# Moving the second block's x load, two table copies, a short index list and one weight copy in the prologue of a CIN kernel

## The chip, the cores and the metric

The kernel runs on one core of one Trainium2 chip. Its time is the device time of one execution in microseconds (us); a kernel's time is the median over several runs. The engines are TensorE (PE, with its weight loads PEld), VectorE (DVE), ScalarE (ACT), GpSimd (POOL) and SyncE (SP). Transfers are issued from ACT, SP and POOL and carried by 16 DMA engines.

## The reference

The model is a compressed interaction network of three layers on `x`, which has 1024 samples, 39 fields and 64 embedding elements. Each layer multiplies its input with the fields, pair by pair and element by element, and mixes the products with a weight matrix:

```python
def _cin_layer(Xk, X0, W, b):
    O = W.shape[0]
    Hk, Fdim = (Xk.shape[1], X0.shape[1])
    Wr = W.reshape(O, Hk, Fdim)
    return jnp.einsum('bhe,bfe,ohf->boe', Xk, X0, Wr) + b[None, :, None]

for W, b in ((W0, b0), (W1, b1), (W2, b2)):
    Xk = _cin_layer(Xk, X0, W, b)
    outs.append(Xk.sum(axis=-1))
cin_output = jnp.concatenate(outs, axis=-1)
return cin_output @ fc_w.T + fc_b
```

W0 is 64 x 1521, W1 and W2 are 64 x 2496. All is float32 and the output is 1024 x 1.

## The kernel before

The pairs of fields are symmetric, so each unordered pair (and each field with a constant row of ones) needs one product. The kernel lays the pairs out over 128 partitions. For each of 32 blocks of samples (2048 columns each, 32 samples by 64 elements) five tiles of 128 rows, `rt[n % 2][:, 0..4]`, hold fields in five different orders. A product `(n, c)` of two of these tiles (`PAIRS`, six of them, c = 0 to 5; line 217, DVE) covers 128 pairs, and a smaller product `(n, 6)` of the tiles U and V (line 219) covers the rest for two blocks at once. PE multiplies each product with a weight chunk `wa[:, c]` (line 557 for c below 6, lines 577 and 588 for the rest) in four quarters of 512 columns, each in two passes, and collects a block in four PSUM banks. At the end of a block ACT and DVE finish the banks (lines 605 to 618).

The order of work is written out by hand: a list `steps` of the products, DVE computing the product four steps ahead of PE (`AHEAD`).

How the tiles are filled: `load(n)` (line 166) copies one block of `x` in 1248 pieces of 256 bytes into a table `xd` in DRAM; a table holds two blocks with, for each, a row of ones behind the 39 fields (`fill_ones`, line 362). `roll(n)` (line 176) makes POOL gather the five tiles of block n from the table by `lists` (line 172; 1 MB each), and `roll_small` gathers U and V (0.5 MB each) by the last two columns of `lists`. Block 0 is special. Its samples arrive as two halves in `xh` (line 249, ACT's queue). Tiles 0 to 3 are gathered straight from the halves, eight gathers of 0.5 MB (lines 383 to 385). Between the fourth and the fifth of them POOL issues `load(1)` (line 387). SP copies the halves on into the table (line 389, two copies of 156 KB). Tile 4 is gathered from the table (`roll(0, (4,))`, line 390), then U and V and the five tiles of block 1 (lines 469 and 470).

The weights are prepared in the prologue. ACT's queue carries W2, the first half of x, W0, W1 and the second half, in this order. PE turns and combines them into PSUM; ACT copies four pieces of W0 into `both` (line 459); DVE transposes four pieces of W1 out of PSUM into `flat` (line 489, called T below), copies of which fill the rest of `both`. From `both` DVE adds up the weight rows (`pairs`, line 524), PE transposes them (line 541) and ACT copies them to `wa` (lines 542 and 543). The masks for W1 (`v2`, line 448) and the integer lists of U and V (lines 465 to 468) are small DVE steps ahead of T.

The products of block 0 for c = 0, 1, 2 are split: their first 1024 columns need the first half's gathers only, the second 1024 columns those of the second half. After them come products (0, 3), (0, 4) and on over all 2048 columns; (0, 4) and (0, 5) are the ones that read tile 4.

## Time and profile before

| what | value |
|---|---|
| median of 3 runs | 734.55 us (734.49 to 734.55) |
| the profiled execution's own time | 734.99 us |
| its span, first to last instruction | 733.2 us |
| PE busy | 727.5 us (99%) |
| DVE busy | 638.9 us (87%) |
| POOL busy | 377.6 us (51%) |
| ACT busy | 167.7 us (23%) |
| granted TensorE clock | 1.000 |
| first product pass of PE (line 557) | at 17.02 us of the span |

A row of the page's fifth part gives a line, an engine, what is written and read, the count, the busy time with the mean of one instruction, and the idle time of the engine just ahead with what ended it. In the timeline and in the chain each row begins with the start in us from the span's start and the duration in us. A row that ends in `x4` stands for four instructions. "DMA to landing" is the time from the start of a DMA instruction until its transfer has landed.

### The profile page before, as it was taken

To read this page: it belongs to the slowest core of one execution; us is meant where nothing else is said; L and a number is where in the kernel's file an instruction comes from. 1 tells how busy PE (TensorE), PEld (TensorE's weight loads), DVE (VectorE), ACT (ScalarE), POOL (GpSimd) and SP (SyncE) were. 2 spreads that over 40 slices of the span, in tenths; PEclk is the share of its full clock that TensorE was granted. 3 is DMA by queue.
4 is the path that set the end of the run, shared out by engine and by line. 5 is a ranking of instruction groups with operands and counts; after the bars stand their busy time and mean duration, and the time that the engine had idled before them with its cause. 6 is when DMAs were issued, how large, how long until landed. Compare 5 with 4: busy or idle time off the path is not lost.

```text
span 733.2 us, 6352 instructions
## 1 busy us (share of the span) xinstructions
PE 727.5 (99%) x2377; PEld 314.9 (43%) x2377; DVE 638.9 (87%) x520; ACT 167.7 (23%) x241; POOL 377.6 (51%) x254
## 2 busy tenths in 40 slices
PE   9999999999999999999999999999999999999998
PEld 4344444444444444444444444444444444444443
DVE  6998889988889888898988889888898888889885
ACT  3332121222212222121221212221122221212222
POOL 6858754537555455654547545455654447535300
PEclk9999999999999999999999999999999999999999
DMA  8999967779585796757778676886767876566700
GB/s 264 419 296 381 377 263 276 282 286 323 223 279 238 287 354 261 264 236 265 310 286 299 236 286 228 313 347 224 274 244 276 314 286 259 201 270 245 287 0 1
DMA packets 65979, 197.23 MB, mean 269 GB/s; under 512 B 40109, under 2 KB 40174, under 8 KB 45980
## 3 DMA queue, kind: packets, MB, share of 16 engines
q0 software_dynamic: 28784, 185.56, 65.5%
q1 hardware_dynamic: 35464, 9.28, 5.5%
q10 hardware_dynamic: 1700, 1.99, 0.9%
q8 instruction: 18, 0.29, 0.2%
q14 instruction: 13, 0.11, 0.0%
HBM read 196.76 MB, written 10.60 MB: 283 GB/s over the span
## 4 chain that ended last, share of the span: by engine, by line
PE 97%; DMA 1%; POOL 1%; DVE 1%; issue 0%; ACT 0%; DVEq 0%
PE po L557 90%; PE po L577 4%; PE po L588 2%; DMA r<-xh,lists 1%; POOL r L172 1%; PE idle L276 0%; PE pv L399 0%; DVE p L217 0%; POOL xd L166 0%; PE tr L541 0%; DVE g L607 0%; DVE sums L629 0%; ACT z L605 0%; PE small L320 0%; DVE blocks L420 0%
## 5 line engine op out<-in xcount | busy, mean ns | idle before, releaser
L557 PE MATMUL po<-p,wa 128*128 128x512 f32 x1536 | 665.9, 594 | 0.7 <-DVE p L217 0.5
L217 DVE TENSOR_TENSOR p<-r 128x2048 f32<-128x2048 f32 (+2 forms) x197 | 434.4, 2236 | 74.2 <-PE po L557 72.7
L557 PEld LDWEIGHTS po<-p,wa 128*128 128x128 f32 x1536 | 289.6, 190 | 371.5 <-issue 348.5
L172 POOL DMA_INDIRECT r<-xd,lists x156 | 299.6, 1920 | 289.9 <-issue 275.2
L605 ACT ACTIVATE z<-po,columns 64x512 f32<-64x512 f32 x128 | 87.4, 683 | 375.0 <-PE po L588 220.1
L607 DVE SCALAR_TENSOR_TENSOR g<-po,b0s,z 64x512 f32<-64x512 f32 x128 | 95.9, 749 | 9.3 <-ACT z L605 5.3
L600 ACT COPY g<-r 39x1024 f32<-39x1024 f32 x64 | 66.7, 1043 | 149.2 <-DVE sums L618 120.4
L618 DVE TENSOR_REDUCE sums<-g 103x16 f32<-103x1024 f32 x62 | 75.6, 1220 | 2.1
L172 POOL DMA_INDIRECT u<-xd,lists x16 | 30.3, 1891 | 5.0 <-issue 4.6
L172 POOL DMA_INDIRECT v<-xd,lists x16 | 29.7, 1854 | 4.9 <-issue 4.9
L577 PE MATMUL po<-p,wa 32*64 32x512 f32 x512 | 31.6, 600 | 0.0
L219 DVE TENSOR_TENSOR p<-u,v 128x1024 f32<-128x1024 f32 x16 | 19.5, 1217 | 0.0
L577 PEld LDWEIGHTS po<-p,wa 32*64 32x64 f32 x512 | 9.4, 131 | 20.2 <-issue 20.2
L588 PE MATMUL po<-u,wa 32*64 32x512 f32 x256 | 17.0, 587 | 0.0
L172 POOL DMA_INDIRECT r<-xh,lists x8 | 8.1, 1006 | 4.6 <-DVE blocks L420 2.5
L588 PEld LDWEIGHTS po<-u,wa 32*64 32x64 f32 x256 | 5.7, 132 | 8.0 <-issue 8.0
L276 PE MATMUL idle<-const-float32-1.0 128*128 128x512 f32 (+2 forms) x12 | 6.7, 649 | 0.8 <-PEq L790 0.8
L524 DVE TENSOR_TENSOR pairs<-both 128x2 f32<-128x2 f32 (+27 forms) x59 | 6.1, 171 | 0.1
L542 ACT COPY wa<-tr 128x128 f32<-128x128 f32 x8 | 2.1, 266 | 15.4 <-PE tr L541 15.4
L166 POOL DMA_DIRECT2D xd<-in_x x3 | 3.2, 1070 | 0.0
L276 PEld LDWEIGHTS idle<-const-float32-1.0 128*128 128x128 f32 x12 | 2.6, 257 | 1.0 <-issue 0.7
L541 PE MATMUL tr<-unit,pairs 128*128 128x128 f32 x8 | 2.3, 287 | 0.6 <-ACT wa L543 0.5
(96 smaller groups left out, 56.5 us busy)
## 6 DMA issues: line engine op xcount, KB each, us to landing
xd<-in_x SPq DMA_DIRECT2D x28, 312.0 KB
r<-xd,lists POOLq DMA_INDIRECT x156, 9.1
xd<-in_x POOLq DMA_DIRECT2D x3, 312.0 KB, 7.7
w2s<-in_w ACTq DMA_DIRECT2D x1, 624.0 KB
w1s<-in_w ACTq DMA_DIRECT2D x1, 624.0 KB
w0s<-in_w0t ACTq DMA_DIRECT2D x1, 380.2 KB
xh<-in_x ACTq DMA_DIRECT2D x2, 156.0 KB
xd<-xh SPq DMA_DIRECT2D x2, 156.0 KB
```

The source lines that it names most:

```text
L172: nc.gpsimd.indirect_dma_start(dst, None, table, bass.IndirectOffsetOnAxis(ap=lists[:, k : k + 1], axis=0))
L217: nc.vector.tensor_tensor(p[:, cols], r[:, i, cols], r[:, k, cols], ALU.mult)
L219: nc.vector.tensor_tensor(p[:, 0:SUB], ut[n // 2 % 2], vt[n // 2 % 2], ALU.mult)
L276: nc.tensor.matmul(idle[:, 0:cols], nc.const_aps.tensor(1.0, (128, 128), F32), nc.const_aps.tensor(1.0, (128, cols), F32), start=True, sto ...
L524: nc.vector.tensor_tensor(out, diagonal(a, b, sa, sb), diagonal(b, a, sb, sa), ALU.add)
L557: nc.tensor.matmul(po[n][m], wa[:, c, side : side + 2 * H], p[:, bass.ts(m, MM)], start=n % 2 == 0 and c == 0, stop=n % 2 == 1 and c == NP ...
L577: nc.tensor.matmul(dst[half * H : half * H + H], wa[rows, NPAIR, at : at + H], p[rows, bass.ts(side, MM)], start=t >= 2, stop=t < 2 and ha ...
L588: nc.tensor.matmul(dst[half : half + H], wa[rows, NPAIR + 1, H : 2 * H], ut[n // 2 % 2][rows, bass.ts(side, MM)], start=False, stop=t < 2,)
L600: nc.scalar.copy(gt[H : H + F], rt[n % 2][0:F, 0, bass.ts(m, SUB)])
L605: nc.scalar.activation(z[one], po[n][m][other], AF.Identity, bias=fc0s[other])
L607: return lambda: nc.vector.scalar_tensor_tensor(g[n][m // 2][0:H, at], po[n][m][one], b0s[one], z[one], ALU.add, ALU.mult)
L618: nc.vector.tensor_reduce(sums[:, b_at : b_at + SB], g[n][m // 2].rearrange("p (b e) -> p b e", e=E), AX.X, ALU.add,)
```

## The change

Four things move, all in the prologue.

1. `load(1)` is issued by ACT right behind the second half of x, instead of by POOL between its gathers.
2. SP's two copies of the halves into the table, and with them POOL's gather of tile 4, U, V and block 1, stand behind T in the program. SP reaches them only after a new transfer: the ones of the third table are now written by SP from a new tile `ones2`, which DVE sets right behind T; before, POOL wrote them from `ones` behind its gathers.
3. The four DVE steps that make U's and V's lists stand ahead of the masks.
4. Of the four copies of W0's pieces, DVE makes the second one, ACT the other three.

```diff
+    ones2 = const.tile([64, 2, 32], F32, name="ones2")
...
         load_half(1)
+        load(1, nc.scalar)
...
         for k, cols in enumerate(halves):
             for i in range(4):
                 gather_rows(rt[0][:, i, cols], xh[k], i)
-            if not k:
-                load(1, nc.gpsimd)
-        for k in (1, 0):
-            nc.sync.dma_start(xd[0][0:F, halves[k]], xh[k])
-        roll(0, (4,))
...
         fused(most, r, 4.0, most, ALU.add, ALU.add)
+        nc.vector.tensor_tensor(seat, seat, far, ALU.add)
+        nc.vector.tensor_tensor(both_of[:, 0:1], most, jumps[:, 0:1], ALU.add)
+        nc.vector.tensor_tensor(both_of[:, 1:2], both_of[:, 0:1], jumps[:, 1:2], ALU.add)
+        nc.vector.tensor_scalar(lists[:, 2 * NT :], both_of, 2.0, seat, ALU.mult, ALU.add)
...
         for k, n in enumerate((8, 5)):
             for t in range(2):
                 m = (n + 1 - t) // 2
-                nc.scalar.copy(
+                copy = nc.vector.tensor_copy if (k, t) == (0, 1) else nc.scalar.copy
+                copy(
...
-        nc.vector.tensor_tensor(seat, seat, far, ALU.add)
-        nc.vector.tensor_tensor(both_of[:, 0:1], most, jumps[:, 0:1], ALU.add)
-        nc.vector.tensor_tensor(both_of[:, 1:2], both_of[:, 0:1], jumps[:, 1:2], ALU.add)
-        nc.vector.tensor_scalar(lists[:, 2 * NT :], both_of, 2.0, seat, ALU.mult, ALU.add)
-        roll_small(0)
-        roll(1)
...
-        fill_ones(2, nc.gpsimd, ones)
...
             nc.vector.transpose(
                 flat[:, k], pt[k][:, 0 : 32 * NA].rearrange("p (h f) -> p f h", f=NA)
             )
+        nc.vector.memset(ones2, 1.0)
+        nc.sync.dma_start(
+            xd[2][F::FT].rearrange("r (p c) -> p r c", c=32), ones2
+        )
+        for k in (1, 0):
+            nc.sync.dma_start(xd[0][0:F, halves[k]], xh[k])
+        roll(0, (4,))
+        roll_small(0)
+        roll(1)
...
```

More of the change, by code (lines that the diff above doesn't have):

```diff
@@ L464, in cin_kernel @@
                 )
-        nc.vector.tensor_tensor(seat, seat, far, ALU.add)
-        nc.vector.tensor_tensor(both_of[:, 0:1], most, jumps[:, 0:1], ALU.add)
-        nc.vector.tensor_tensor(both_of[:, 1:2], both_of[:, 0:1], jumps[:, 1:2], ALU.add)
-        nc.vector.tensor_scalar(lists[:, 2 * NT :], both_of, 2.0, seat, ALU.mult, ALU.add)
-        roll_small(0)
-        roll(1)
-        for h in (0, H):
-            nc.gpsimd.dma_start(b0s[h : h + H], b0.rearrange("(h o) -> h o", o=1))
-        for k, t in enumerate((b1, b2)):
-            nc.gpsimd.dma_start(bias[:, k : k + 1], t.rearrange("(h o) -> h o", o=1))
-        nc.gpsimd.dma_start(fcb, fc_b.rearrange("(p o) -> p o", o=1))
-        fill_ones(2, nc.gpsimd, ones)
         w1v = w1s.rearrange("o (h f) -> o h f", f=F)
@@ L491, in cin_kernel @@
             )
+        nc.vector.memset(ones2, 1.0)
[7 more added lines that the diff above has]
+        roll(1)
+        for h in (0, H):
+            nc.gpsimd.dma_start(b0s[h : h + H], b0.rearrange("(h o) -> h o", o=1))
+        for k, t in enumerate((b1, b2)):
+            nc.gpsimd.dma_start(bias[:, k : k + 1], t.rearrange("(h o) -> h o", o=1))
+        nc.gpsimd.dma_start(fcb, fc_b.rearrange("(p o) -> p o", o=1))
         for k, a in groups:
```

## The prediction

> **What bounds the kernel now.** I read the page first, then the chain that ended last, then the timelines of DVE and POOL over the first 40 us, the landing of single gathers, and a table of 2 us stretches.

> ```profile
> PE 727.5 (99%) x2377; PEld 314.9 (43%) x2377; DVE 638.9 (87%) x520; ACT 167.7 (23%) x241; POOL 377.6 (51%) x254
> PE po L557 90%; PE po L577 4%; PE po L588 2%; DMA r<-xh,lists 1%; POOL r L172 1%; PE idle L276 0%; PE pv L399 0%; DVE p L217 0%; POOL xd L166 0%; PE tr L541 0%; DVE g L607 0%; DVE sums L629 0%; ACT z L605 0%; PE small L320 0%; DVE blocks L420 0%
> ```

> PE carries nine tenths of the path. The change touches no pass of PE's, so what it can move lies ahead of the stretch where PE runs without a gap. The chain says where that begins:

> ```profile
> 11.80 1.07 POOL xd L166
> 12.87 0.30 issue
> 13.18 0.98 POOL r L172
> 14.16 0.31 issue
> 14.47 8.09 DMA r<-xh,lists
> 22.56 0.03 issue
> ...
> 22.65 1.24 DVE p L217
> ...
> 24.02 4.53 PE po L557 x10
> ```

> Up to 24.02 the end hangs on POOL's issues, with load(1) (line 166) among them, on the second gather of the second half (issued at 14.47, landed at 22.56) and on the DVE product that waits for it. The DVE timeline shows the wait, and what follows it:

> ```profile
> 20.25 1.21 DVE L217 TENSOR_TENSOR p<-r 128x1024 f32<-128x1024 f32 x1
> 22.65 3.68 DVE L217 TENSOR_TENSOR p<-r 128x1024 f32<-128x1024 f32 x3 [1.20 <-DMA r<-xh,lists]
> 26.25 1.05 DVE L524 TENSOR_TENSOR pairs<-both 128x28 f32<-128x28 f32 x11
> 27.23 2.27 DVE L217 TENSOR_TENSOR p<-r 128x2048 f32<-128x2048 f32 x1
> 29.43 0.79 DVE L524 TENSOR_TENSOR pairs<-both 128x22 f32<-128x22 f32 x7
> 30.14 2.28 DVE L217 TENSOR_TENSOR p<-r 128x2048 f32<-128x2048 f32 x1
> ```

> The reader is to see the 1.20 us of idle at 22.65, and that DVE has none from there on. The DMA engines are full meanwhile, by the shares in the last columns but one:

> ```profile
> 14.00:16.00 2.00, 2.00 (x11) 0.81 (x10) 1.80 (x8) 1.37 (x5) 1.39 (x3) 1.00 0.94 320
> 18.00:20.00 2.00, 1.90 (x6) 0.67 (x4) 2.00 (x10) 0.38 (x2) 1.69 (x2) 1.00 1.02 401
> 22.00:24.00 2.00, 1.56 (x4) 0.39 (x3) 1.34 (x2) 1.82 (x5) 1.39 (x3) 1.00 1.05 426
> ```

> **What a us of that wait is worth.** A pass takes 0.431 us (41.40 us for 96 in the chain). PE's last pass on the first half begins at 22.54 by its weight load, so the next could begin at 22.97; it begins at 24.02: 1.05 us lost. Product (0, 3) ends at 29.51 and holds PE again: passes begin at 28.39 and 28.50, the next could at 28.93 and comes at 29.62. So a second half that lets DVE go x earlier moves PE by x, up to the 1.20 us of the wait. Later PE runs through: it reaches (0, 4) at about 33.3 (six passes behind 30.69), while DVE ends that product at 32.42, 0.85 us ahead.

> **Load(1) on ACT's queue.** POOL loses one issue of 1.08 us, so its four second-half gathers issue 1.08 us earlier. The transfer is not gone: it follows the second half of x (landed at 9.77, when SP's wait for it ends) in pieces of 256 bytes, which the packet records price at 18 ns; 1248 of them are 1.4 us of all 16 engines. It leaves POOL's queue, where it took 1.2 us (landings 18.35 of the fourth gather, 19.52 of load(1)), and falls among the first-half gathers. These landed at 12.0, 13.5, 17.0 and 18.4; DVE reads them at 16.13, 16.13, about 18.2 and 20.25. The first two have over 2.5 us to spare, the third 1.2, the fourth 1.9; the third also loses SP's copies ahead of it. So no loss there. U waits for load(1), but now is issued later than it lands. ACT itself pays the issue: 0.78 us by SP's usual row of the same load, 8.92 us by its worst (the one behind a full queue, at 24.96). ACT is idle 3.81 us before its first W0 copy at 9.94, so up to 3.8 us are hidden. I take 1 us: nothing.

> **Copies behind T.** T ends at 14.83, the new memset some 0.1 us later (the 128x64 memset takes 0.11). SP then issues the ones (0.34 by the row of the other ones), copies at about 15.4 and 16.3 instead of 9.77 and 10.70. The copies carry 78 packets of 4 KB at 0.20 us: 1.0 us of 16 engines, out of the way of the first half. They took 6.3 and 6.5 us from issue to landing by the semaphore records, so they land near 21.7 and 22.8, and their packets may start at 18 to 19.5: partly still ahead of the second-half gathers. Sum for the second gather of that half: less 1.0 (copies), less 1.2 (load(1) on POOL), plus up to 1.4 (load(1) on ACT), plus 0 to 1.0 (the copies again). It lands 0.8 us earlier to 0.2 us later; the pace of issue allows 1.1. I take 0.45 us, nearer the middle, for x; its ends are -0.2 and 1.1.

> **What the copies hold up.** POOL's gather of tile 4 waits for them, and U, V and all of block 1 stand behind it on POOL.

> ```profile
> 18.58 1.66 POOL L172 DMA_INDIRECT r<-xd,lists  x1 [0.31 <-issue]
> 20.66 1.61 POOL L172 DMA_INDIRECT u<-xd,lists  x1 [0.42 <-DVE pairs L524]
> ```

> Tile 4 goes at 18.58 now and lands 9.0 us later, at 27.6. After the change it goes when the second copy has landed, between 20.3 (first packets 1.5 us after the issue, as for SP's loads later in the packet records, and 2.5 us for the copy) and 22.8. With the queue drained a 1 MB gather lands in 7.6 us (the gather at 63.03), with a full one in 9.0:

> ```profile
> DMA to landing us min/median/max: 7.6/7.6/7.6
> DMA to landing us min/median/max: 9.0/9.0/9.0
> ```

> So tile 4 lands between 27.8 and 31.8; I take 29.8 (22 plus 7.8). DVE would reach (0, 4) at 29.7, and PE suffers only when tile 4 lands after 30.14 + 0.85 = 31.0, less the gain: hidden, but the cover shrinks from 2.5 us to about nothing. The rest moves up to 3 us: block 1's second tile landed at 35.4 and PE needs product (1, 0) at 44.0, 2.3 us of DVE later: 6 us of cover. U and V (28.9 and 30.2, read at 35.99, by PE at 41.26) have over 4.

> **The small steps.** The lists move from 9.83 into DVE's 1.22 us of idle before the masks at 9.55, four steps in 0.7 us there: nothing. DVE's W0 copy waits for ACT's first one (ends near 10.5) and takes about ACT's 0.55 us, inside DVE's 1.49 us of idle that end at 12.04: nothing either way; ACT ends 0.5 us sooner, but then waits for T. The memset stands between T and the copy at 14.86, on DVE's way to the first product: +0.07 us. SP's first ones for the second table still wait for ACT at 23.66. POOL no longer issues the third table's ones at 38.21; its next gather waits until 45.15 for other things: nothing.

> **Sum.** -0.45 + 0.07 = -0.4 us. The profiled execution, 734.99 us (span 733.2 and 1.8 around it), becomes 734.6; it stands 0.44 us above the median, so the median becomes 734.15. 0.2% is 1.47 us, about what a measurement of this kernel can tell from no change.

> [...] The trace's packets show 256-byte pieces from SP's queue passing one for one with POOL's large packets from 28 to 40 us (some 47 and 50 per us). [...]

> **Rivals.**
> (1) The full gain: copies and load(1) out of the way let the second half land before 21.45; DVE's whole wait goes. -1.2 + 0.07 gives 733.4. For it: copies take no packet until about 19. Against it: the DMA share of 0.94 to 1.04, the same bytes.
> (2) Slower: tile 4 takes the place of the wait. From a landing at 31.0 on, each us is a us; at the upper bound, 31.8, it costs 0.8 us (735.4), and if copies crawl behind both other queues for 2 us more, 2.8 us (737.3).
> (3) ACT's queue is full and load(1)'s issue blocks it. From 3.8 us on the W0 copies are late, from 4.8 on T (DVE's copy waits for ACT's). At the worst row, 8.92 us, T is 4 us late: 738.6. Against it: the five issues there took 0.83 us at most, and two of their transfers are done by 6.
> (4) Bytes only change places: 734.6.

> **How the numbers follow.** The forecast with (4), 733.8 to 734.9, has 0.45; (1), 0.22; (2), 0.19, two fifths of it beyond 736.0; (3), 0.08; the rest, 0.06, goes in halves to gains I see no row for and to late first-half gathers. The cases give faster by over 0.2% 0.10 (a quarter of (1), reached when the passes behind it close up too, and half the rest), slower 0.19 (the part of (2), (3), half the rest), same 0.71. The range runs from 733.2 to 736.8: it takes in (1) and (2) nearly to its end, and leaves out (3).

> **What would show it.** Right: DVE's wait before the second half shrinks to 0.5 to 1.0 us, PE's second-half pass begins near 23.5, tile 4's gather issues after 20 and no DVE wait stands before (0, 4). Wrong: an ACT table load later than 7 us, a first W0 copy later than 10, a DVE idle of over 1 us near 30 behind tile 4, or a first product later than 16.3.

## The result: 0.4% slower, and the profile after

The changed kernel takes 736.81 us (median of 736.65 to 738.4) against 734.52 us for the kernel before on the same chip: a ratio of 1.0041, 95% interval 1.003 to 1.0052. Measured on two more occasions the ratio was 1.0039 (1.0026 to 1.0052) and 1.005 (1.0033 to 1.0067). So it is slower, by about 2 to 3 us.

The first profiled execution took 736.7 us with a span of 734.9 us. Its page has the same work as before; PE's busy time differs by 0.7 us, part of it passes at half clock:

```profile
PE 728.2 (99%) x2377; PEld 315.8 (43%) x2377; DVE 639.5 (87%) x522; ACT 167.1 (23%) x240; POOL 387.6 (53%) x252
```

DVE's timeline in it (start, duration, in brackets the idle time before and what ended it):

```profile
20.12 4.63 DVE L219 TENSOR_TENSOR p<-r 128x1024 f32<-128x1024 f32 x4
...
30.64 2.29 DVE L219 TENSOR_TENSOR p<-r 128x2048 f32<-128x2048 f32 x1 [1.99 <-DMA r<-xd,lists]
...
41.27 2.29 DVE L219 TENSOR_TENSOR p<-r 128x2048 f32<-128x2048 f32 x1 [3.57 <-DMA r<-xd,lists]
```

The four products of the second half now run in one piece: the 1.20 us of waiting are gone, all of them. In their place stand 1.99 us before (0, 4), where there was no wait, and 3.57 us before (1, 0). SyncE's and POOL's timelines show where these come from:

```profile
14.63 0.71 SPq L481 DMA_DIRECT2D xd<-ones  x1
15.46 1.71 SPq L485 DMA_DIRECT2D xd<-xh  x2
```

```profile
22.83 2.87 POOL L172 DMA_INDIRECT r<-xd,lists  x1 [6.53 <-DMA xd<-xh]
26.01 2.88 POOL L172 DMA_INDIRECT u<-xd,lists  x1 [0.30 <-DVE pairs L526]
```

The copies go at 15.46 and 16.49. POOL stands still for 6.53 us until they have landed, issues tile 4 at 22.83 (18.58 before), and that gather lands at 30.5 (27.6 before). Meanwhile there is nothing for the DMA engines to do, as the 2 us stretches show (last three columns: clock, DMA share, GB/s):

```profile
20.00:22.00 2.00, 2.00 (x4) 0.86 (x3) 2.00 (x5) 0.38 (x2) 0.00 (x0) 0.50 0.41 166
22.00:24.00 2.00, 2.00 (x5) 0.71 (x4) 2.00 (x3) 0.54 (x3) 1.17 (x1) 0.76 0.00 0
24.00:26.00 2.00, 2.00 (x6) 0.95 (x5) 2.00 (x13) 1.98 (x3) 1.70 (x1) 1.00 0.01 4
```

In the stretch from 22 to 24 us they were full before (1.05). The column of the clock shows something else: half clock from 19.55 to 22.96. The chain of what ended last has its source, a report of PE's that ACT gets late. (A report stands here for the semaphore update that the trace records for an ended instruction; `idle` is the tile that the passes of `spin` write and nobody reads, so `PE idle` is work and no pause.)

```profile
16.56 1.78 PE idle L279 x2
18.34 0.26 ACT wa L544
...
18.64 1.21 PE po L559 x2
19.85 0.21 PE tr L543
20.06 3.22 PE po L559 x4
```

PE turned the first weights at 16.27, ACT copied them only at 18.34, and the first product pass came at 18.64 instead of 17.02. The semaphore's own records agree: three reports come together, between 18.27 and 18.34, for passes that ended between 16.2 and 17.0. After that PE ran without a gap in this execution, at half speed for 3.41 us. Its last product pass is 1.34 us later than before (729.03 against 727.69). So this profile has two things in it, an emptied DMA queue and late reports, and PE pays here for the second. It isn't the whole story of the six executions: the longest, 738.4 us, had a mean granted clock of 0.999, while one stretch of 3.41 us at half clock takes the mean to 0.998. The experiments had to tell the two apart.

### The profile page after: what moved, and what is told of

Same layout as the page of the kernel before. It is cut to its first block, busy times and chain, and to the rows that moved or that the text cites. A ratio compares the mean times of both kernels' runs of the same rounds, so it can differ in the third digit from the quotient of the medians.

```text
span 734.9 us, 6355 instructions
## 1 busy us (share of the span) xinstructions
PE 728.2 (99%) x2377; PEld 315.8 (43%) x2377; DVE 639.5 (87%) x522; ACT 167.1 (23%) x240; POOL 387.6 (53%) x252
## 4 chain that ended last, share of the span: by engine, by line
PE 99%; DVE 0%; ACT 0%; issue 0%
PE po L559 90%; PE po L579 4%; PE po L590 2%; PE idle L279 1%; PE pv L394 0%; PE pt L468 0%; PE pw L406 0%; PE small L323 0%; PE tr L543 0%; PE pv L468 0%; DVE g L609 0%; DVE sums L631 0%; ACT z L607 0%; PE pv L432 0%; ACT wa L544 0%
## 5 line engine op out<-in xcount | busy, mean ns | idle before, releaser
L172 POOL DMA_INDIRECT r<-xd,lists x156 | 302.2, 1937 | 284.0 <-issue 268.7
L607 ACT ACTIVATE z<-po,columns 64x512 f32<-64x512 f32 x128 | 87.4, 683 | 374.4 <-PE po L590 219.6
L172 POOL DMA_INDIRECT v<-xd,lists x16 | 39.0, 2438 | 4.9 <-issue 4.9
L172 POOL DMA_INDIRECT u<-xd,lists x16 | 30.3, 1895 | 4.9 <-issue 4.3
L221 DVE TENSOR_TENSOR p<-u,v 128x1024 f32<-128x1024 f32 x16 | 19.5, 1219 | 0.0
L172 POOL DMA_INDIRECT r<-xh,lists x8 | 7.7, 959 | 4.1 <-issue 2.1
L631 DVE TENSOR_REDUCE sums<-g 103x8 f32<-103x512 f32 x4 | 2.7, 686 | 0.1
```

What stands on the lines that cost most here:

```text
L172: nc.gpsimd.indirect_dma_start(dst, None, table, bass.IndirectOffsetOnAxis(ap=lists[:, k : k + 1], axis=0))
L221: nc.vector.tensor_tensor(p[:, 0:SUB], ut[n // 2 % 2], vt[n // 2 % 2], ALU.mult)
L607: nc.scalar.activation(z[one], po[n][m][other], AF.Identity, bias=fc0s[other])
```

## The experiments

The theories: **A**, load(1) on ACT's queue holds up PE's reports; **B**, the late copies on SyncE's queue hold them up; **C**, the half clock is most of the loss; then **D**, the loss is POOL's wait for the late copies, which makes tile 4 and block 1 late, against **E**, it is the late report with the half clock behind it; and later **F**, **G** (tile 4's share against block 1's), **H** (the start of PE's clock) and **S** (small writes). Times in brackets behind a median are the shortest and the longest execution.

**load(1) on ACT alone**, on the kernel before:

```
+        load(1, nc.scalar)          # behind load_half(1)
-            if not k:
-                load(1, nc.gpsimd)
```

> Only load(1) moves to ACT's queue; the copies stay where they were. Theory A (the small pieces of load(1), run early and fast, are what holds back PE's reports between 16 and 18 us): the stall ahead of the first product pass is there, the pass comes at 18 us or later instead of 17.0, the granted clock has a stretch at half, and the time is 735.5 to 737. Theory B (the late copies on SP's queue are what holds them back): no stall, a first pass near 17.0, clock 1.000, and a gain of 0.3 to 1.1 us from POOL's earlier issue: 733.4 to 734.3.

734.38 us (732.43 to 735.99) against 734.56, ratio 0.9995 (0.9985 to 1.0006). No report is late, so on this chip A falls, and the wait before the second half is gone:

```profile
21.47 4.62 DVE L217 TENSOR_TENSOR p<-r 128x1024 f32<-128x1024 f32 x4
```

The time is the same. In this profile PE's full clock came at 15.11 us instead of 13.05 and the first product pass at 18.25 instead of 17.02; from the first pass to the last PE needed 709.6 us instead of 710.7. So it gained 1.1 us where the wait had been and had lost as much ahead of it. In the total the gain isn't told from nothing; the interval, whose lower end is a gain of 1.1 us, doesn't rule it out either.

**The copies' move alone** (with the ones, and POOL's gathers of tile 4, U, V and block 1 behind them):

```
-        for k in (1, 0):                                  # behind the gathers of the halves
-            nc.sync.dma_start(xd[0][0:F, halves[k]], xh[k])
-        roll(0, (4,))
+        nc.vector.memset(ones2, 1.0)                      # behind T's transposes
+        nc.sync.dma_start(xd[2][F::FT]..., ones2)
+        for k in (1, 0):
+            nc.sync.dma_start(xd[0][0:F, halves[k]], xh[k])
+        roll(0, (4,)); roll_small(0); roll(1); ...
```

> Only the copies, tile 4, U, V and block 1's gathers move behind T, with the ones of the third table on SP; load(1) stays on POOL. Theory A: no stall, clock 1.000; the second half lands up to 1 us earlier, tile 4 near 30.5, so DVE waits some 2 us before product (0, 4): 734.0 to 735.0. Theory B: the stall ahead of the first pass is there with a stretch at half clock: 736 to 737.

735.97 us (733.42 to 739.31), ratio 1.0029 (1.0012 to 1.0047), with full clock and no late report in its profile, so B falls on this chip too. The loss is there all the same, and more than A's expectation allowed; the longest execution, 739.31 us, had a mean clock of 1.000. DVE's timeline:

```profile
30.63 2.29 DVE L218 TENSOR_TENSOR p<-r 128x2048 f32<-128x2048 f32 x1 [0.87 <-DMA r<-xd,lists]
...
39.87 2.29 DVE L218 TENSOR_TENSOR p<-r 128x2048 f32<-128x2048 f32 x1 [2.18 <-DMA r<-xd,lists]
43.45 2.29 DVE L218 TENSOR_TENSOR p<-r 128x2048 f32<-128x2048 f32 x1 [1.28 <-DMA r<-xd,lists]
...
50.36 1.52 DVE L611 SCALAR_TENSOR_TENSOR g<-po,b0s,z 64x512 f32<-64x512 f32 x2
```

and PE's:

```profile
58.21 1.99 PE L561 MATMUL po<-p,wa 128*128 128x512 f32 x4 [0.31 <-DVE p L218]
```

Block 1's gathers stand behind tile 4's on POOL and land later too. DVE's waits there push its part of finishing block 0's banks, finish(0), to 50.36, and (1, 4) behind it holds PE: 0.91 us between the starts of two passes at 57.30 and 58.21, where a pass takes 0.43. In the kernel before finish(0) and (1, 4) stood here:

```profile
45.93 1.52 DVE L607 SCALAR_TENSOR_TENSOR g<-po,b0s,z 64x512 f32<-64x512 f32 x2
...
51.44 4.48 DVE L217 TENSOR_TENSOR p<-r 128x2048 f32<-128x2048 f32 x2
```

By the ratios this one part makes most of the loss by itself. The profiled execution, 735.42 us, is one of the shorter ones; what the longer ones lost in isn't shown.

**Lists and W0 copy alone.**

> Only the lists ahead of the masks and the one W0 copy on DVE. Both theories: no stall, T within 0.1 us of 12.04, time within 0.3 us of before. A stall here would say that neither transfer is its cause.

734.52 us, ratio 0.9995 (0.9985 to 1.0005): nothing, as predicted.

**Keeping the clock up**: in the changed kernel a longer run of the passes of `spin` behind the first turned weights.

```
-            spin()
+            spin(2, MM)
```

> The changed kernel with four idle passes of 512 columns instead of two of 256 behind PE's first transpose of pairs; they fill PE until the first product. Theory C (of the 2.3 us, 1.7 is the half clock that PE gets for 3.41 us after idling, and the rest the wait itself): the clock stays 1.000 and the time falls by 1.3 to 1.8 us, to 735.0 to 735.5. Rival: the passes only delay the first product or the clock drops all the same: 736.6 to 737.5.

736.79 us (734.46 to 737.85), ratio 1.0024 (1.0009 to 1.0038). No late report and full clock in its profile; yet DVE waits 2.39 us before (0, 4) and 3.21 before (1, 0), and PE waits for (0, 4) and near 58 for (1, 4):

```profile
33.20 1.10 PE L559 MATMUL po<-p,wa 128*128 128x512 f32 x2 [1.01 <-DVE p L219]
```

The kernel is slower than the one before without the half clock as well: C falls. Whether the half clock adds to the loss isn't told by this; the changed kernel itself wasn't run on this chip.

**The changed kernel profiled again**, on another chip:

> The changed kernel again. Theory D (the loss is POOL's wait of some 6.5 us for the late copies: tile 4 and block 1's gathers land late, DVE waits 2 us before (0, 4) and 3 us before (1, 0), and PE waits for (0, 4) or (1, 4)): the DVE waits are there as before, 735.5 to 737. Theory E (the loss is the stall ahead of the first product pass and the half clock behind it): a stretch of 3.41 us at half clock between 16 and 24 us is there again. If the stall is absent and the time is the same, E falls as the main cause.

737.95 us (737.64 to 738.17), ratio 1.0039. No late report and full clock throughout. The view of waits (total, times, longest):

```profile
POOL r L172 <- DMA xd<-xh: 8.0, 1, 8.0
...
DVE p L219 <- DMA r<-xd,lists: 6.2, 3, 3.8
...
PE po L559 <- DVE p L219: 2.7, 1, 2.7
```

Here PE's full clock came at 14.48, T ended near 15.6, the copies went at 16.56 and 17.52 and landed at 23.36 and 24.19; tile 4 went at 24.95 and landed at 33.44. DVE waited 3.8 us for it and PE 2.7 us for DVE:

```profile
24.95 1.85 POOL L172 DMA_INDIRECT r<-xd,lists  x1 [7.97 <-DMA xd<-xh]
...
36.01 1.10 PE L559 MATMUL po<-p,wa 128*128 128x512 f32 x2 [2.66 <-DVE p L219]
```

PE's passes of the smaller product (`join` in the kernel, line 588 before, 590 here) ended 2.81 us later than before and the last product pass 2.81 us later: what is lost at (0, 4) stays to the end. On this chip D holds (the time came out above its 735.5 to 737) and E falls as the main cause.

**The changed kernel without the copies' move**:

> The changed kernel without its second part: load(1) on ACT's queue, lists and W0 copy moved, copies on SP as soon as the halves land. Theory D: POOL does not wait for the copies, tile 4 lands before 27, no DVE wait before (0, 4) or (1, 0); 733.5 to 734.5. Theory E in the form that early load(1) brings the stall: half clock between 16 and 24 us and 736 or more.

734.16 us (733.6 to 736.1), ratio 0.9995 (0.9986 to 1.0004), on the same chip as the run just shown: the loss is gone. The expectation was missed at block 1:

```profile
39.75 2.29 DVE L217 TENSOR_TENSOR p<-r 128x2048 f32<-128x2048 f32 x1 [4.84 <-DMA r<-xd,lists]
```

```profile
17.01 2.38 POOL L172 DMA_INDIRECT r<-xd,lists  x1 [0.89 <-issue]
19.70 5.27 POOL L172 DMA_INDIRECT u<-xd,lists  x1 [0.30 <-DVE pairs L524]
```

U's gather needed 5.27 us on POOL, beside DVE's products without a pause; the last section comes back to it. Two passes of PE start 1.47 us apart near 56 by it, so some 1.0 us is lost.

**The copies some 4 us earlier** in the changed kernel: memset, ones and copies ahead of T's transposes instead of behind them.

> The changed kernel with the memset, the ones and the copies issued ahead of T's four transposes instead of behind them: the copies go some 3.4 us earlier, near 12, and all that waits for them too. Theory D: tile 4 lands near 27, DVE waits less than 0.5 us before (0, 4) and less than 1 us before (1, 0), PE waits for neither; 733.5 to 734.6. If the time stays above 735.5, the lateness of the copies is not what costs.

735.49 us (733.1 to 737.02), ratio 1.0005 (0.9996 to 1.0015). POOL and DVE in the profiled execution, one of the shortest (733.3 us):

```profile
20.26 0.94 POOL L172 DMA_INDIRECT r<-xd,lists  x1 [3.75 <-DMA xd<-xh]
```

```profile
35.83 2.29 DVE L219 TENSOR_TENSOR p<-r 128x2048 f32<-128x2048 f32 x1 [0.92 <-DMA r<-xd,lists]
```

Tile 4 lands at 26.47, nothing waits for it, and no product holds PE. The time missed its expectation of 733.5 to 734.6 and stands just under the 735.5 that would have spoken against D. By the ratios, the earlier the copies, the smaller the loss: 0.4% behind T, 0.05% (not told from nothing) some 4 us earlier, nothing at their old place.

**Tile 4 from the halves**, so that it waits for no copy; only U, V and block 1 do:

```
         for i in range(4):
             gather_rows(rt[0][:, i, cols], xh[k][0:F], i)
+    for k, cols in enumerate(halves):
+        gather_rows(rt[0][:, 4, cols], xh[k], 4)          # xh has a row of ones now
-    roll(0, (4,))
```

in the changed kernel; in the version with early copies; in the version with the copies 4 us earlier:

> The changed kernel, with one thing more: tile 4 of block 0 no longer comes from the table that the copies fill, but from the two halves of x, as the other four tiles do (two gathers of 512 KB behind the second half's; the halves get a row of ones early on SyncE). So tile 4 waits for no copy, and only U, V and block 1 stand behind the copies as in the changed kernel. Theory F (tile 4's late landing is nearly all of the loss): tile 4 lands before 29, no DVE wait before (0, 4), PE's wait there of 1.0 to 2.7 us is gone, last product pass near 727.5, time 734.0 to 735.3, ratio to before at most 1.0010. Theory G (block 1's late gathers cost as much by themselves): POOL still waits some 6 us for the copies, DVE waits over 1.5 us before (1, 0), PE waits 0.9 us or more for (1, 4) near 57, last pass 728.3 or later, time 735.6 or more, ratio 1.0020 or more. A third: two gathers more among the second half's make the second half late, DVE waits over 1 us near 21 and the passes there come later.

> As the changed kernel without its copies' move (lists, W0 copy and load(1) on ACT only), with tile 4 of block 0 from the halves. Nothing stands behind the copies but U, V and block 1, and the copies are early. Theory F and G both: no DVE wait before (0, 4); U's issue comes earlier than in the version without the move, whose DVE waited 4.84 us before (1, 0) because U's issue on POOL took 5.27 us beside DVE's products. If U's issue still runs beside the products, that wait stays at 3 to 5 us with PE's gap of 0.9 to 1.5 us near 56 (734.0 to 734.6); if it gets done in the pauses, wait and gap go (733.0 to 733.8).

> The changed kernel with ones and copies ahead of the transposes that end T (some 4 us earlier than behind them), and tile 4 of block 0 from the halves. Theory F: nothing is left of the loss and the second half's gain stays: 733.2 to 734.2, ratio 0.9985 to 0.9998. Theory G: block 1's gathers still come late (DVE waits before (1, 0) of about 1 us), but PE does not wait: 734.0 to 734.9, ratio within 0.0005 of 1.

736.15 us (732.3 to 737.38), ratio 1.0016 (1.0001 to 1.0031); 734.94, ratio 1.0012 (0.9998 to 1.0025); 735.37 (732.08 to 736.88), ratio 1.0012 (1.0001 to 1.0022). The profiled executions were among the shortest (733.16, 733.85, 732.33 us) and show what F hoped for: no wait before (0, 4), last passes at 725.61, 726.24 and 724.78. But the times of one kernel spread over some 5 us, while the kernel before stayed within 733.5 and 735.5 beside them. F and G can't be judged by that, and none of the three beats the kernel before.

**The spread**: two of these kernels and the kernel before profiled again, on another chip.

> The changed kernel with tile 4 from the halves, profiled again. Theory H (when PE's clock is granted in full decides): in the execution profiled first the clock was full from 8.2 us, the copies went at 13.3 and POOL waited for nothing: 733.16 us. An execution whose clock comes at 12 us or later has T's end near 15 and copies that land at 22 to 24; POOL then waits for them and DVE before (1, 0) for 4 us or more, PE for (1, 4): 735.5 to 737.5 us. One with the clock before 10 us again gives 732.3 to 733.5. Against H: a time over 735.5 with the clock before 10 us, or a time under 734 with the clock after 12.

> Copies ahead of T's last transposes, tile 4 from the halves, profiled again. Theory H: the first profile had the clock from 8.5 us and 732.33 us. With the clock at 12 us or later PE's first pass and the copies are 2 to 3 us later; DVE waits 2 us or more before (1, 0), PE 0.5 us or more near 55: 734.9 to 736.9 us. With the clock before 10 us: 732 to 733.3.

> As the second look at this kernel: 735.5 to 737.5 us with the clock full at 12 us or later, 732.3 to 733.5 with the clock before 10 us; theory H falls if the time does not follow the clock's start.

> The kernel before, profiled again on this chip, to see how much its own time follows the clock's start. Theory H says little: its copies and its gather of tile 4 wait for nothing on PE, so with the clock at 8 us or at 14 the time is 733.5 to 735.5, DVE's wait for the second half is about 1.2 us less whatever T is late by, and the last pass lies within 1 us of 727.7.

739.73, 741.28, 739.75 and 734.21 us. H falls as the whole account: the version with the earlier copies had its full clock at 7.28 us and took 741.28. What the three longer ones show is the late report of the first profile, longer. It doesn't explain all of the spread above: there the changed kernel with tile 4 from the halves took 737.25 and 737.38 us in two executions with a mean clock of 1.000. That spread stays open. ACT, in the changed kernel with tile 4 from the halves (739.73 us):

```profile
21.27 0.27 ACT L549 COPY wa<-tr 128x128 f32<-128x128 f32 x1 [6.43 <-remote]
```

and PE in its 2 us stretches (the length of the stretch, PE's busy time and instructions, then PE's weight loads, DVE, ACT and POOL, and as above):

```profile
16.00:18.00 2.00, 0.45 (x3) 0.04 (x1) 2.00 (x11) 0.00 (x0) 1.39 (x3) 1.00 1.04 405
18.00:20.00 2.00, 0.00 (x0) 0.00 (x0) 1.58 (x10) 0.00 (x0) 1.61 (x1) 0.57 1.04 406
```

PE turned the first weights at 15.71. Four of its reports are recorded together, between 21.18 and 21.30. PE stood for 5.14 us and had half clock for 6.83 us, from 18.29 on. In the kernel before on that chip:

```profile
15.98 0.27 ACT L542 COPY wa<-tr 128x128 f32<-128x128 f32 x1 [1.03 <-PE idle L276]
```

the report came 0.3 us after its pass began.

**Without SyncE's small writes** (128 pieces of 128 bytes for the third table's ones), beside the changed kernel and the one with tile 4 from the halves, on that same chip:

```
-        nc.vector.memset(ones2, 1.0)
-        nc.sync.dma_start(xd[2][F::FT]..., ones2)
+        fill_ones(2, nc.gpsimd, ones)                     # on POOL, behind fcb
```

> The changed kernel again, as the measure for the next one on the same chip: 736.5 to 738.4 us. Of interest is whether PE's reports come late between 15 and 22 us, as in its first profile (2 us) and in the three later looks (5 to 6 us), or not, as in its second.

> The changed kernel without the memset and SyncE's ones for the third table (128 pieces of 128 bytes) behind T; the ones go from POOL late, as before. The copies are some 0.9 us earlier than in the changed kernel, the rest is the same. Theory S (those small writes hold up the engines' reports): no late report in the trace even where the changed kernel on the same chip has one, and 0.5 to 2 us less. Theory of the late copies alone: reports late or not as in the changed kernel; tile 4 some 0.9 us earlier, time 0.3 to 1 us less than the changed kernel's, still over 735.5.

> The changed kernel with tile 4 from the halves, beside the one without SyncE's ones: 732.3 to 737.4 where reports are in time, some 739.7 where they come 5 us late.

> As the one before, without SyncE's ones for the third table (POOL writes them late). Theory S: no late reports, 732.3 to 735 us on any chip. If late reports come with it as well as without, the small writes are not the cause.

737.16 (ratio 1.005), 737.5 (734.55 to 744.07, ratio 1.0043, 1.0013 to 1.0073), 737.88 (1.005) and 740.39 us (1.0076). In the changed kernel's profile the first report is late by some 0.8 us, the clock is full, DVE waits 2.06 us before (0, 4), and PE waits 0.91 us there and 0.91 us for (1, 4): D's waits again. S falls: both versions without the small writes have a late report, ACT in the first of them:

```profile
20.61 0.27 ACT L540 COPY wa<-tr 128x128 f32<-128x128 f32 x1 [5.46 <-remote]
```

The expectation was wrong about the copies as well. They themselves have nothing to do with T; they stood behind the ones in SyncE's queue, and the ones wait for a memset that DVE reaches after T. With the ones gone the copies went at 9.21 and tile 4 early:

```profile
16.60 1.25 POOL L172 DMA_INDIRECT r<-xd,lists  x1 [0.59 <-issue]
```

No product of block 0 waits for a transfer in that profile, and the execution still took 739.33 us. So the late report is a loss of its own, which needs no late copies. This version moves what the changed kernel without the copies' move moves, and that one lost nothing on its chip (ratio 0.9995): on this chip the same changes cost 0.43%. Three executions of this version with at most a short half-clock stretch (granted mean of 0.998 to 1.0) took 734.55 to 735.09 us, as the kernel before; the six at 0.995 and below, 737.06 to 744.07.

## Why the prediction was wrong

**Load(1) on ACT.** Right that it costs ACT nothing (first W0 copy at 9.65, so rival 3 fell). The gain x was mis-sized: 0.45 us taken, the whole 1.20 us of DVE's wait measured, as rival 1 had it. The term "plus up to 1.4 (load(1) on ACT)" was the error: the 1248 pieces passed between 8 and 10 us, when some 805 pieces went a us, before the gathers' packets filled the engines, so they took nothing from the second half. With load(1)'s move alone the second gather of that half landed at 20.23 instead of 22.56. What the wait costs PE was misread as well: 22.54 and 28.39 are starts of weight loads, which run ahead of their passes (the load at 22.54 belongs to the pass at 22.97). PE's own rows before:

```profile
20.61 2.95 PE L557 MATMUL po<-p,wa 128*128 128x512 f32 x6
24.02 4.53 PE L557 MATMUL po<-p,wa 128*128 128x512 f32 x10 [0.47 <-DVE p L217]
```

The last of the six passes begins at 22.97, so the next could at 23.40: 0.62 us lost, not 1.05, and at 29.65 it is 0.29 us, not 0.69. In the total the removed wait showed no measurable time by itself.

**What the copies hold up.** This is the step that failed: the cost of the late copies, put at nothing because tile 4 was to land in time ("hidden"). Its terms in us, where the first profile is that of the result and the second the one on another chip:

| | predicted | copies' move alone | first profile | second profile |
|---|---|---|---|---|
| second copy issued | 16.3 | 16.55 | 16.49 | 17.52 |
| second copy landed | 22.8 | 23.52 | 22.07 | 24.19 |
| POOL issues tile 4 | 22 | 24.25 | 22.83 | 24.95 |
| tile 4 landed | 29.8 | 30.51 | 30.52 | 33.44 |

Tile 4 goes behind the second copy, and the prediction took 22 though it had that copy landing at 22.8. From the landing to POOL's issue 0.73 to 0.76 us passed each time, a term that the sum hadn't. A copy took 6.7 to 7.0 us to land instead of 6.3 to 6.5 (5.6 in the first profile, where some updates aren't recorded), and T, from which everything counts, was 0.8 us late in the second profile, where PE's full clock came late. The gather then took 6.3 to 8.5 us, where 7.8 was taken. "The cover shrinks from 2.5 us to about nothing" put the forecast at the edge of a cliff and gave only 0.19 to falling off it. Its rule held: with a landing 2.4 us after 31.0, PE lost 2.8 us, and with one at 30.5 it lost 0.25 us there. In the first profile itself PE paid for the late report and not for this step, since it came to (0, 4) only after DVE had finished it.

**"6 us of cover" for block 1** left out finish(0). DVE has 5.5 us of it (four sums, two reductions) between (1, 3) and (1, 4), and PE needed (1, 4) at 57.85 before, which DVE had finished at some 53.7: 4.1 us of cover. And "the rest moves up to 3 us" was too little: with the copies' move alone block 1's five tiles landed 4.4 to 5.4 us later (37.27 to 48.31 against 32.81 to 43.05) and finish(0) began 4.4 us later. That uses the cover up: passes near 58 start 0.84 to 1.50 us apart, where they take 0.43, in three profiles.

**The small steps** cost nothing, as said. The forecast of 734.15 was wrong, rival 2 came true in its mechanism: tile 4 takes the place of the wait. Its upper end of 737.3 agrees with the 2.8 us of the second profile by luck: it stood for copies that crawl for 2 us more, while here a copy took 0.2 to 0.5 us longer than the sum had it, and the rest came from T, the 22, POOL's issue and the gather. Of the signs listed, the one against the forecast came: an idle DVE of over 1 us near 30 behind tile 4.

**What no step had**: PE's reports that come 0.8 to 5 us late, mostly with half a clock behind. They were in the result's profile, whose chip isn't on record, and in all profiles of changed versions on one chip, all with load(1) on ACT; on the three other chips on record no profile has them, with load(1) on ACT or without. The kernel before had none in its two profiles. In the profiles with late reports few semaphore updates are recorded from 8 to 18 us (1 to 6 a us in that of the result, 4 to 30 in the first of the kernel before) and then a burst, but the kernel before has gaps of that kind on the same chip without a late report. What brings them on stays open: load(1) on ACT alone wasn't tried on that chip. They aren't needed for the verdict: on the chips whose profiles show none the copies' move alone costs 0.29% and the changed kernel 0.39%. On the chip that has them the copies' share isn't separated.

## What to carry to other kernels

A transfer that others gather from isn't placed by the engines' load alone: count from its issue to its landing (6.7 to 7.0 us here), then the gather's own time (6.3 to 8.5 us), and ask for the cover of everything that stands behind it in the same queue, one stage further than the first consumer. A queue's order is a dependency: the copies waited for T only because a small write ahead of them in SyncE's queue did (they went at 15.73 us with it and at 9.21 without it, on one chip). And a wait that has been removed from an engine off the critical path is worth what PE's passes gain, here 1.1 us in one profile and nothing that the total could show.

## What the runs showed of the hardware

**POOL's issues stop beside DVE's products.** An indirect gather takes POOL 0.94 us to issue where DVE pauses, 5.27 us (19.70 to 24.97) beside 4.6 us of products in one piece, and 12.48 us (55.61 to 68.09 in the first profile) beside products in one piece from 56.19 on. So a DVE that waits less makes POOL issue later: that is what took back block 1's lead in the version with early copies. U's issue ended 0.95 us after the four products did, about the length of an unhindered one. Not every issue beside products is held: in the kernel before three that began 0.04 to 0.08 us ahead of a product (22.58, 23.82 and 25.07) took 0.94 us each beside products from 22.65 to 26.33. What holds the others isn't shown.

**PE's full clock starts between 7.28 and 15.11 us** in the profiles given here, and differently in executions of one kernel: 12.72, 14.48 and 13.43 us in the changed one, 8.21 to 14.58 in the one with tile 4 from the halves. T moves with it (its end in the changed kernel at 14.5, 15.6 and 14.8 us), and whatever is hung behind T: in that last one the first copy went at 13.28 us in the profile with the earliest clock and at 16.83 in that with the latest.
